# Two graph-attention layers: the logits of a pair side by side, layer 1's edge weights handled per pair and turned through HBM

## The chip, the cores and the metric

The kernel runs on one NeuronCore of one Trainium2 chip. The metric is the device time of one execution in microseconds (us), lower is better. All arithmetic is fp32. Five instruction streams matter: the PE (TensorE: matmuls and transposes into PSUM), DVE (VectorE), ACT (ScalarE), POOL (GpSimd) and SP, the queue that issues nearly all DMAs. Each executes its own list strictly in the order in which it was written.

## The reference, cut to what matters

x is 128 batches of 128 nodes with 512 features, adj 128 batches of a 128 x 128 integer matrix. Layer 0 is masked attention with 8 heads of 64, layer 1 a graph attention with one head:

```python
q, k, v = x @ Wq + bq, x @ Wk + bk, x @ Wv + bv            # 8 heads of 64
attn = softmax(where(adj > 0, q @ k.T / 8, -1e9))          # per batch and head, 128 x 128
x = layernorm(x + relu((attn @ v) @ Wo + bo))
Wh = x @ W
e = leaky_relu((Wh @ a1)[:, None] + (Wh @ a2)[None, :], 0.2)
attention = softmax(where(adj == 0, -1e9, e))              # per batch, 128 x 128
out = layernorm(x + elu(attention @ Wh))
```

The kernel computes `attention @ (x @ W)` as `(attention @ x) @ W`, and gets `Wh @ a1` and `Wh @ a2` from two vectors `W @ a` that it folds once at the start.

## The kernel before

**Tiling.** The 128 batches are worked on as 64 pairs; pair p is batches 2p and 2p+1. The products with Wq, Wk, Wv, Wo and W take the pair's two batches as the two rows of blocks of one 2 x 2 block product, and do it with 7 block products in place of 8 (`PRODUCTS`, L137; the sums of blocks that this needs are `left_sums`, L145, for the left side and `weight_sums`, L129, for the weights). The seven products go to three PSUM banks A, B and C, which accumulate one upon the other: a bank is read by DVE or ACT between two products (`qk_p1`, `qk_p6`, `v_p6`, `w_p6`, `o_c11` and so on), and the PE may only add the next product when that read is done. Here `qk` is the product with Wq and Wk together, `v`, `o` and `w` are those with Wv, Wo and W; `qk3` is the fourth product of `qk`.

**Stages of a pair.** `load_blocks` and `x_transpose` bring x in transposed form. `qk0` to `qk6` and `v0` to `v6` follow. `logits` (L396) writes 128 x 1024 logits of one batch to two PSUM banks, `mask_logits` and `max_logits` (DVE), `exp_logits` and `norm_logits` (ACT) make the softmax. The weights are then transposed: DVE turns 32 x 32 blocks (`weights_t`, L437), a DMA writes the result to HBM (`weights_out`, L443), four DMAs read it back in transposed block order (`weights_in`, L448). `mix_values` (L456) multiplies by v into one PSUM bank, and ACT copies it out. After `o`, `residual0`, `stats0` to `norm0` make the layer norm. The edge stage of layer 1 works batch by batch: `edge_term` (dot products with the folded vectors), `edge_row` (a PE transpose of a broadcast column), `edge_sums`, `edge_leaky`, `edge_mask`, `edge_max`, `edge_exp`, then `edges_t` (L525), a PE transpose of the 128 x 128 weights, and `edges_t_out` (L529), its copy by ACT. `mix_nodes` (L533), `w0` to `w6`, the elu, a residual and the second layer norm finish the pair, and `store` writes it.

**What sets the order.** `PLAN` (L19) gives each step a due time relative to its pair; step k of pair p gets the key `p * PERIOD + PLAN[k]`, all are sorted, and the queues are filled in that order (L574 to L625). The plan's numbers are therefore only an order: the place of a step within a period is its value modulo `PERIOD`, and the number of whole periods in it says how many pairs later than `logits` it comes. Before, `mix_values` to `mix_nodes` of a pair come one period after its logits, and `w` two periods after.

**PSUM.** There are 8 banks: `ps_att` has one buffer of two banks for logits (L80), `ps_acc` the banks A, B, C (L81), `ps` three buffers of one bank (L82) that `mix_values`, `edge_row`, `edges_t`, `mix_nodes` and the folding share.

**Order on the PE before**, within one period in the steady state: `mix_nodes`, `logits0`, both `mix_values`, `logits1`, then `v4` to `v6`, `w` and `o` interleaved, `qk`, with the `edge_row` and `edges_t` transposes among `qk` and the `v0` to `v3` of the next pair.

**Loads of weights.** `load_block_x` (L122) issues two DMAs per 256 x n block, each for 128 partitions, with a source of 4 x 32 rows. Wq and Wv are issued from ACT's queue, all else from SP's (L170 to L184).

Of the kernel before, what the change touches and what calls it, by code (L numbers as in the profile page):

```python
# [17 lines left out]
PERIOD = 80.36  # L18
PLAN = dict(  # L19
    load_blocks=-203.35, load_adj=-141.65, x_transpose0=-108.79, x_transpose1=-80.72, sums_qk=-62.62, mask=-35.32,  # L20
    sums_v=-33.81, x_sums=-30.87, qk0=-30.03, qk_p1=-28.89, qk1=-24.47, qk_p1q=-23.84, qk_p6=-23.67, qk4=-22.15,
    qk3=-21.47, qk2=-20.46, qk_p7=-19.06, qk_c11=-17.42, qk_c22=-16.69, qk5=-15.77, v0=-13.29, sums_fold0=-12.95,
    v_p1=-11.35, fill_logits1=-10.97, qk6=-9.66, qk_c21=-9.52, v1=-8.33, v2=-7.72, v_p6=-6.99, v3=-6.55,
    fill_logits0=-4.19, qk_c12=-2.81, sums_o=-1.37, logits0=0.0, v_p7=1.78, mask_logits0=6.87, logits1=6.98,
    v4=8.58, v_c11=11.52, max_logits0=11.75, mask_logits1=12.17, v_c22=12.53, v5=17.32, max_logits1=17.42,
    v_c21=18.18, v6=18.57, v_c12=18.66, exp_logits0=26.37, sum_logits0=28.64, exp_logits1=31.22, norm_logits0=33.91,
    fill_edges0=36.7, sums_fold1=37.99, sums_fold_t0=42.14, sum_logits1=47.8, load_x0=56.09, norm_logits1=56.91,
    weights_t0=57.44, sums_fold_out0=60.06, weights_out0=61.6, weights_in0=62.47, sums_fold_t1=65.58,
    weights_t1=67.46, sums_fold_out1=74.55, mix_values0=81.46, weights_out1=82.7, weights_in1=84.68,
    mix_values1=87.22, mix_values_out0=94.58, mix_values_out1=96.97, sums_w=98.84, o_sums=103.62, o0=108.53,  # L30
    load_x1=109.41, o_p1=114.18, fill_edges1=114.73, o1=117.76, o_p1l=118.1, o2=120.61, o_p6=122.66, o3=122.75,
    o_p7=123.47, o4=123.68, o_c11=126.83, o_c22=129.32, o5=129.79, o_c21=130.83, residual01=132.36, o6=132.67,
    o_c12=133.46, stats01=133.46, mean01=133.56, residual00=134.07, rstd01=136.55, stats00=137.12, shift01=137.46,
    mean00=137.78, norm01=137.87, rstd00=137.95, edge_term01=138.68, edge_term11=139.19, shift00=140.27,
    norm00=141.75, edge_term10=142.12, edge_term00=142.31, edge_row1=143.18, edge_sums1=143.88, edge_row0=145.26,
    edge_leaky1=147.3, edge_sums0=147.37, edge_mask1=149.05, edge_leaky0=150.02, edge_max1=150.22,
    edge_mask0=151.47, edge_max0=152.05, edge_exp1=152.16, edge_exp0=152.23, edge_norm1=152.34, edges_t1=152.35,
    edges_t0=154.18, edges_t_out1=154.18, edge_norm0=154.29, mix_nodes1=154.39, edges_t_out0=154.42,
    mix_nodes0=154.6, mix_nodes_out1=156.09, mix_nodes_out0=157.89, z_sums=164.73, w0=173.41, w1=179.87,
    w_p1=181.52, w_p6=182.07, w2=182.1, w3=185.01, w_p7=187.54, w4=187.83, w_c11=188.88, w_c22=190.51, w5=195.11,  # L40
    w6=195.64, w_c21=198.1, elu_exp1=198.84, w_c12=200.38, elu_low1=215.59, elu_max1=222.2, elu_exp0=222.5,
    elu_low0=228.48, residual11=235.55, elu_max0=240.61, stats11=243.8, mean11=247.72, rstd11=249.46,
    residual10=251.29, shift11=265.27, stats10=269.96, mean10=297.04, finish1=299.37, rstd10=315.64, store1=320.24,
    shift10=323.36, finish0=332.2, store0=341.53)
# [4 lines left out]
    xb=2, adj=4, xT=3, sx=2, pr=2, e1a512=1, e1b512=1, mask=1, u2512=1, u3512=2, qT=2, kT=2, e1a256=2, cv=2,  # L49
    u2256=1, u3256=1, t=2, scr=2, cw=4, prb=1, prT=2, oT=2, x=2, at=3, so=1, e1b256=2, co=5, e=2, attT=7, zT=2,  # L50
# [4 lines left out]
def tile_two_graph_layers(ctx: ExitStack, tc: tile.TileContext, x, adj, wq, bq, wk, bk, wv, bv, wo, bo, w, a, out,  # L55
# [24 lines left out]
    ps_att = ctx.enter_context(tc.tile_pool(name="ps_att", bufs=1, space=bass.MemoryType.PSUM))  # L80
    ps_acc = ctx.enter_context(tc.tile_pool(name="ps_acc", bufs=1, space=bass.MemoryType.PSUM))  # L81
    ps = ctx.enter_context(tc.tile_pool(name="ps", bufs=3, space=bass.MemoryType.PSUM))  # L82
# [6 lines left out]
    XB, PRB, PRD, NMEAN = {}, {}, {}, {}  # L89
# [32 lines left out]
    def load_block_x(t, k, queue, src, rows, cols):  # L122

        for c in range(2):
            queue.dma_start(t[:, k, c, :], bass.AP(
                tensor=src.tensor, offset=src.offset + 32 * (2 * rows + c) * D + cols.start,
                ap=[[P * D, 4], [D, 32], [1, cols.stop - cols.start]]))
# [48 lines left out]
    load_blocks(1)  # L176
    load_adj(1)
    wv_b, wo_b, w_b = (block_weight(n, HALF) for n in ("wv", "wo", "w"))
    for t, src, queue, load in ((wv_b, wv, nc.scalar, load_block_x), (wo_b, wo, nc.sync, load_block),
                                (w_b, w, nc.sync, load_block)):  # L180
        load(t, 0, queue, src, 0, lo)
        load(t, 5, queue, src, 0, hi)
        load(t, 1, queue, src, 1, lo)
        load(t, 2, queue, src, 1, hi)  # L184
# [211 lines left out]
    def logits(p, i):  # L396
        b = 2 * p + i
        q, k = (QK[m, b].rearrange("r (h n) -> r h n", n=P) for m in "qk")
        ST["s", b] = ps_att.tile([P, 2, H // 2, P], F32, tag="att", name=f"s_{b}")
        for hp in range(H // 2):  # L400
            for j in range(2):
                r = slice(j * DH, (j + 1) * DH)
                nc.tensor.matmul(ST["s", b][:, j, hp, :], q[r, hp, :], k[r, hp, :], start=True, stop=True)  # L403
# [33 lines left out]
    def weights_t(b):  # L437

        PRB[b] = buf([P, 4, H, 32], F32, "prb", f"prb_{b}")
        nc.vector.transpose(PRB[b].rearrange("p k h s -> p h k s"),  # L440
                            PR.pop(b).rearrange("p h (k r) -> p h k r", r=32))

    def weights_out(b):  # L443

        PRD[b] = hbm.tile([P, 4, H * 32], F32, tag="prd", name=f"prd_{b}")
        nc.sync.dma_start(PRD[b], PRB.pop(b).rearrange("p k h s -> p k (h s)"))

    def weights_in(b):  # L448

        PRT[b] = buf([P, 4, H, 32], F32, "prT", f"prT_{b}")  # L450
        prd = PRD.pop(b)
        for k in range(4):
            nc.sync.dma_start(PRT[b][32 * k:32 * k + 32].rearrange("r v h s -> r v (h s)"),
                              prd[:, k, :].rearrange("(v r) e -> r v e", v=4))
# [31 lines left out]
    def edge_term(b, s):  # L486
        store = (EI, EJ)[s]
        store[b] = small.tile([P, 1], F32, tag=f"e{s}", name=f"e{s}_{b}")
        scr = buf([P, D], F32, "scr", f"scr{s}_{b}")
        nc.vector.scalar_tensor_tensor(scr, X1[b], 1.0, wa_bc[s], op0=ALU.mult, op1=ALU.mult, accum_out=store[b])  # L490


    def edge_row(b):
        ST["j", b] = ps.tile([P, P], F32, tag="ps", name=f"pj_{b}")
        nc.tensor.transpose(ST["j", b], EJ.pop(b).to_broadcast([P, P]), ident)

    def fill_edges(b):
        AT[b] = buf([P, P], F32, "at", f"at_{b}")
        nc.gpsimd.memset(AT[b], NEG)

    def edge_sums(b):
        ST["e", b] = buf([P, P], F32, "e", f"e_{b}")
        nc.scalar.activation(ST["e", b], ST.pop(("j", b)), AF.Identity, bias=EI.pop(b), scale=1.0)

    def edge_leaky(b):
        e = ST["e", b]
        nc.vector.scalar_tensor_tensor(e, e, ALPHA, e, op0=ALU.mult, op1=ALU.max)

    def edge_mask(p, i):
        b = 2 * p + i  # L510
        nc.vector.copy_predicated(AT[b], ADJ[p][:, i, :], ST.pop(("e", b)))

    def edge_max(b):
        NMAX["e", b] = small.tile([P, 1], F32, tag="nmax1", name=f"nmax1_{b}")
        nc.vector.tensor_reduce(NMAX["e", b], AT[b], AX.X, ALU.max, negate=True)

    def edge_exp(b):
        TOT["e", b] = small.tile([P, 1], F32, tag="tot1", name=f"tot1_{b}")
        nc.scalar.activation(AT[b], AT[b], AF.Exp, bias=NMAX.pop(("e", b)), scale=1.0, accum_out=TOT["e", b])

    def edge_norm(b):
        RI[b] = small.tile([P, 1], F32, tag="ri", name=f"ri_{b}")
        nc.vector.reciprocal(RI[b], TOT.pop(("e", b)))

    def edges_t(b):  # L525
        ST["at", b] = ps.tile([P, P], F32, tag="ps", name=f"pat_{b}")
        nc.tensor.transpose(ST["at", b], AT.pop(b), ident)

    def edges_t_out(b):  # L529
        ATT[b] = buf([P, P], F32, "attT", f"attT_{b}")  # L530
        nc.scalar.copy(ATT[b], ST.pop(("at", b)))

    def mix_nodes(b):  # L533

        attT = ATT.pop(b)
# [13 lines left out]
    def elu_exp(b):  # L549
        t = buf([P, D], F32, "t", f"t_{b}")  # L550
        ST["t", b] = t
        nc.scalar.activation(t, Y[b], AF.Exp, scale=RI[b])  # L552
# [5 lines left out]
    def elu_max(b):  # L558
        nc.vector.scalar_tensor_tensor(Y[b], Y[b], RI.pop(b), ST.pop(("t", b)), op0=ALU.mult, op1=ALU.max)
# [21 lines left out]
    for p in range(n_pair):  # L581
        if p > 1:
            at("load_adj", p, load_adj, p)
            at("load_blocks", p, load_blocks, p)
        at("x_sums", p, x_sums, p)
# [64 lines left out]
```

## Time and profile before

| | |
|---|---|
| time, median of 3 runs | 2511.69 us (2510.5 to 2513.35) |
| span of the profiled execution | 2509.6 us, mean granted PE clock 0.989 |
| busy: PE | 2413.6 us, 96% |
| busy: DVE, ACT, POOL | 1912.0, 1607.5, 1459.9 us |
| share of 16 DMA engines used by SP's queue | 32.3% |
| first `logits` matmul | 60.1 us after the start |
| last pair's first `logits` matmul | 2425.2 us |

The page divides the span into 40 slices and gives each engine's busy share per slice in tenths. A row of the timeline gives the start, the length, the engine, the line, the operation with output and inputs, the shape and how many instructions were merged; in brackets stands how long the engine was idle before and what released it. A row of the waits gives the waiting group, what it waited for, the total in us, how often, and the longest. fp32 matmuls appear as two records each. The end of a PE record is modelled, so the distance from one start to the next is the better measure.

### The profile page before, as it was taken

To read this page: it belongs to the slowest core of one execution; us is meant where nothing else is said; L and a number is where in the kernel's file an instruction comes from. 1 tells how busy PE (TensorE), PEld (TensorE's weight loads), DVE (VectorE), ACT (ScalarE), POOL (GpSimd) and SP (SyncE) were. 2 spreads that over 40 slices of the span, in tenths; PEclk is the share of its full clock that TensorE was granted. 3 is DMA by queue.
4 is the path that set the end of the run, shared out by engine and by line. 5 is a ranking of instruction groups with operands and counts; after the bars stand their busy time and mean duration, and the time that the engine had idled before them with its cause. 6 is when DMAs were issued, how large, how long until landed. Compare 5 with 4: busy or idle time off the path is not lost.

```text
span 2509.6 us, 51523 instructions
## 1 busy us (share of the span) xinstructions
PE 2413.6 (96%) x17928; PEld 2190.1 (87%) x17928; DVE 1912.0 (76%) x4031; ACT 1607.5 (64%) x5635; POOL 1459.9 (58%) x2053
## 2 busy tenths in 40 slices
PE   3999999999999999999999999999999999999995
PEld 3898998998998998998998898998988988989984
DVE  3777877877877877877877877877777877878775
ACT  0666666666666666676666666666666666666663
POOL 2356656656656656656656656556556556556554
PEclk8999999999999999999999999999999999999997
DMA  4323323423323323323423423323323323333222
GB/s 133 110 78 98 122 84 102 121 78 108 121 83 104 114 89 104 120 86 101 122 79 106 121 78 108 115 82 110 106 88 113 106 83 118 96 93 119 86 73 72
DMA packets 221076, 252.69 MB, mean 101 GB/s; under 512 B 19920, under 2 KB 170448, under 8 KB 220816
## 3 DMA queue, kind: packets, MB, share of 16 engines
q1 hardware_dynamic: 218896, 246.49, 32.3%
q8 instruction: 144, 2.36, 0.4%
q10 hardware_dynamic: 1584, 2.10, 0.2%
q14 instruction: 116, 0.95, 0.1%
q0 software_dynamic: 336, 0.79, 0.1%
HBM read 148.64 MB, written 100.66 MB: 99 GB/s over the span
## 4 chain that ended last, share of the span: by engine, by line
PE 83%; DMA 7%; DVE 6%; SPq 1%; ACT 1%; issue 1%; POOL 0%; ACTq 0%; POOLq 0%; DVEq 0%
PE pBqk L257 10%; PE pAqk L257 8%; PE pCqk L257 7%; PE pBw L246 7%; PE pBo L246 7%; PE pBv L246 6%; PE pCv L246 5%; PE s L403 5%; PE pAw L246 4%; PE pCw L246 4%; PE pAo L246 4%; PE pCo L246 4%; PE po L462 4%; PE pAv L246 3%; PE pz L538 3%; DMA prT<-prd 3%
## 5 line engine op out<-in xcount | busy, mean ns | idle before, releaser
L556 POOL TENSOR_SCALAR t<-t 128x512 f32<-128x512 f32 x126 | 255.0, 2024 | 414.7 <-ACT t L552 414.7
L426 ACT ACTIVATE pr<-pr,nmax 128x128 f32<-128x128 f32 x1024 | 396.0, 391 | 4.3 <-DVE nmax L420 4.3
L435 ACT ACTIVATE pr<-pr,tot 128x128 f32<-128x128 f32 x1024 | 313.8, 412 | 1.4 <-DVE tot L430 1.4
L257 PE MATMUL pBqk<-sx,wqk 128*128 128x128 f32 x2048 | 251.4, 276 | 22.3 <-DVE wqk L132 19.2
L257 PE MATMUL pAqk<-xT,wqk 128*128 128x128 f32 x2048 | 251.3, 276 | 19.1 <-DVE xT L288 19.1
L257 PEld LDWEIGHTS pBqk<-sx,wqk 128*128 128x128 f32 x2048 | 245.3, 193 | 26.1 <-issue 21.6
L273 POOL TENSOR_SCALAR rstd<-mv 128x1 f32<-128x1 f32 x256 | 81.3, 318 | 318.9 <-DVE mv L270 309.5
L257 PEld LDWEIGHTS pAqk<-xT,wqk 128*128 128x128 f32 x2048 | 245.4, 193 | 22.3 <-DVE xT L288 19.1
L415 DVE COPY_PREDICATED pr<-mask,s 128x1024 f32<-128x1024 int32 x128 | 173.5, 1355 | 112.0 <-PE s L403 112.0
L257 PE MATMUL pCqk<-sx,wqk 128*128 128x128 f32 x2048 | 250.0, 275 | 0.0
L257 PEld LDWEIGHTS pCqk<-sx,wqk 128*128 128x128 f32 x2048 | 244.6, 192 | 3.3
L301 ACT ACTIVATE e1aqk<-pAqk,bk 128x128 f32<-128x128 f32 x256 | 73.1, 368 | 246.1 <-PE pAqk L257 246.1
L426 ACT ACTIVATION_READ_ACCUMULATOR pr<-pr,nmax 128x1 f32 x1024 | 194.6, 190 | 0.0
L490 DVE SCALAR_TENSOR_TENSOR scr<-co,wa_bc 128x512 f32<-128x512 f32 x256 | 188.6, 773 | 1.9 <-ACT co L281 1.9
L274 POOL TENSOR_TENSOR rstd<-rstd,half 128x1 f32<-128x1 f32 x256 | 153.0, 597 | 21.3
L562 POOL TENSOR_TENSOR cw<-cw,co 128x512 f32<-128x512 f32 x126 | 160.0, 1270 | 0.0
L420 DVE TENSOR_REDUCE nmax<-pr 128x8 f32<-128x1024 f32 x128 | 155.7, 1216 | 2.2
L440 DVE STREAM_TRANSPOSE prb<-pr 128x1024 f32<-128x1024 f32 x128 | 156.4, 1222 | 0.6 <-DMA prd<-prb 0.6
L462 PE MATMUL po<-prT,cv 128*64 128x128 f32 x2048 | 134.4, 278 | 22.0 <-DMA prT<-prd 16.4
L278 POOL TENSOR_SCALAR nmean<-mv,rstd 128x1 f32<-128x1 f32 x256 | 135.4, 529 | 26.2
L471 ACT ACTIVATE oT<-po,bv 128x128 f32<-128x128 f32 x512 | 142.7, 383 | 12.1 <-PE po L462 11.5
L403 PE MATMUL s<-kT,qT 64*128 64x128 f32 x2048 | 148.7, 285 | 1.5 <-DVE pr L415 1.5
(150 smaller groups left out, 6155.3 us busy)
## 6 DMA issues: line engine op xcount, KB each, us to landing
prd<-prb SPq DMA_DIRECT2D x128, 512.0 KB
prT<-prd SPq DMA_DIRECT2D x512, 128.0 KB
xb<-in_x_dram SPq DMA_DIRECT2D x256, 128.0 KB
x<-in_x_dram SPq DMA_DIRECT2D x128, 256.0 KB
out_dram<-cw SPq DMA_DIRECT2D x128, 256.0 KB
adj<-in_adj_dram SPq DMA_DIRECT2D x64, 128.0 KB
wqk<-in_L_gnn_Wq_dram ACTq DMA_DIRECT2D x4, 256.0 KB
wv<-in_L_gnn_Wv_dram ACTq DMA_DIRECT2D x8, 128.0 KB
```

The costliest lines, as they stand in the source:

```text
L246: nc.tensor.matmul(out, left_block(left, blk.pair, a_i, c), weight[:, b_i, c, :], start=first and c == 0, stop=j in LAST and c == 1, skip_ ...
L257: nc.tensor.matmul(out[:, f * P:(f + 1) * P], weight[:, b_i, c, f * P:(f + 1) * P], left_block(left, blk.pair, a_i, c), start=first and f ...
L403: nc.tensor.matmul(ST["s", b][:, j, hp, :], q[r, hp, :], k[r, hp, :], start=True, stop=True)
L415: nc.vector.copy_predicated(PR[b], MASK[p][:, i, :].unsqueeze(1).to_broadcast([P, H, P]), ST.pop(("s", b)).rearrange("p j h k -> p (j h) k"))
L420: nc.vector.tensor_reduce(NMAX[b], PR[b], AX.X, ALU.max, negate=True)
L426: nc.scalar.activation(PR[b][:, h, :], PR[b][:, h, :], AF.Exp, bias=nmax[:, h:h + 1], scale=1.0, accum_out=TOT[b][:, h:h + 1])
L435: nc.scalar.activation(PR[b][:, h, :], PR[b][:, h, :], AF.Copy, scale=tot[:, h:h + 1])
L440: nc.vector.transpose(PRB[b].rearrange("p k h s -> p h k s"), PR.pop(b).rearrange("p h (k r) -> p h k r", r=32))
L462: nc.tensor.matmul(ST["o", b][j * DH:(j + 1) * DH, hp, :], v[:, h * DH:(h + 1) * DH], prT[:, :, j * (H // 2) + hp, :], start=True, stop=True)
L490: nc.vector.scalar_tensor_tensor(scr, X1[b], 1.0, wa_bc[s], op0=ALU.mult, op1=ALU.mult, accum_out=store[b])
L556: side_engine(b // 2).tensor_scalar(t, t, 1.0, -1.0, op0=ALU.min, op1=ALU.add)
L562: side_engine(b // 2).tensor_tensor(Y[b], Y[b], X1.pop(b), op=ALU.add)
```

## The change

It does five things.

1. **Logits of a pair adjacent.** `logits` now does both batches in one step, and `ps_att` gets two buffers (four banks), so that the second batch's logits need not wait until the first's were read. `ps` is cut to one buffer for this.
2. **Layer 1's edges per pair.** `edge_row` to `edge_norm` handle both batches in one step. The masking, leaky relu, maximum, fill and reciprocal are one instruction of 256 columns in place of two of 128; the ACT steps and the `edge_row` transposes stay two.
3. **Edge weights turned through HBM.** For all pairs but the last, `edges_t` is one DVE 32 x 32 block transpose of 128 x 256 in place of two PE transposes, `edges_t_out` is a DMA to HBM, and a new `edges_t_in` reads back with four DMAs in runs of 128 bytes. ACT's copies fall away. The last pair keeps the PE. In turn the last pair's attention weights of layer 0 (`weights_t`, `weights_out`) now use PE transposes and copies by DVE and ACT in place of HBM.
4. **Loads of layer 0's weights.** `load_block_x` issues four DMAs of 32 partitions each; the loads of Wv move from ACT's queue to SP's, ahead of pair 1's x.
5. **A new plan** with more distance between a DMA and its reader: the edge stage and `mix_nodes` come two periods after a pair's logits, `w` three. Some buffer counts change.

Order on the PE after, from the new plan modulo its period (number of periods after the pair's logits in brackets): `logits` [0], `mix_values1` [1], `v1`, `v2` [0], `edge_row` [2], `v3`, `v4`, `w0`, `v5`, `v6`, `w1`, `w2`, `w3`, `w4`, `o0`, `w5`, `w6`, `o1`, `o4`, `o3`, `o2`, `o5`, `qk0`, `o6`, `qk1`, `qk2`, `mix_nodes1` [2], `qk3`, `qk4`, `qk5`, `mix_nodes0` [2], `qk6`, `v0`, `mix_values0` [0].

The diff, cut to its core:

```diff
-PERIOD = 80.36
+PERIOD = 75.72
...
-    xb=2, adj=4, xT=3, sx=2, pr=2, e1a512=1, e1b512=1, mask=1, u2512=1, u3512=2, qT=2, kT=2, e1a256=2, cv=2,
-    u2256=1, u3256=1, t=2, scr=2, cw=4, prb=1, prT=2, oT=2, x=2, at=3, so=1, e1b256=2, co=5, e=2, attT=7, zT=2,
+    xb=2, adj=4, xT=2, sx=1, e1a512=1, e1b512=1, u2512=1, pr=2, mask=1, u3512=1, qT=2, kT=2, e1a256=2, t=2, scr=1,
+    cw=6, u2256=1, u3256=2, cv=2, prb=2, x=2, prT=2, oT=2, so=1, e1b256=1, co=6, at=2, e=1, atb=1, attT=1, zT=2,
...
-    ps_att = ctx.enter_context(tc.tile_pool(name="ps_att", bufs=1, space=bass.MemoryType.PSUM))
+    ps_att = ctx.enter_context(tc.tile_pool(name="ps_att", bufs=2, space=bass.MemoryType.PSUM))
...
-    ps = ctx.enter_context(tc.tile_pool(name="ps", bufs=3, space=bass.MemoryType.PSUM))
+    ps = ctx.enter_context(tc.tile_pool(name="ps", bufs=1, space=bass.MemoryType.PSUM))
...
-        for c in range(2):
-            queue.dma_start(t[:, k, c, :], bass.AP(
-                tensor=src.tensor, offset=src.offset + 32 * (2 * rows + c) * D + cols.start,
-                ap=[[P * D, 4], [D, 32], [1, cols.stop - cols.start]]))
+        for q in range(4):
+            queue.dma_start(t[32 * q:32 * q + 32, k, :, :], bass.AP(
+                tensor=src.tensor, offset=src.offset + (q * P + 64 * rows) * D + cols.start,
+                ap=[[D, 32], [32 * D, 2], [1, cols.stop - cols.start]]))
...
-    load_blocks(1)
-    load_adj(1)
...
-    for t, src, queue, load in ((wv_b, wv, nc.scalar, load_block_x), (wo_b, wo, nc.sync, load_block),
-                                (w_b, w, nc.sync, load_block)):
+    for t, src, load in ((wv_b, wv, load_block_x), (wo_b, wo, load_block), (w_b, w, load_block)):
+        load(t, 0, nc.sync, src, 0, lo)
...
+        if t is wv_b:
+            load_blocks(1)
+            load_adj(1)
...
-    def logits(p, i):
-        b = 2 * p + i
+    def logits(p):
+        for b in (2 * p, 2 * p + 1):
...
     def weights_t(b):
+        if b // 2 == n_pair - 1:
+            ST["w", b] = ps_att.tile([P, H, P], F32, tag="att", name=f"ppT_{b}")
+            for h in range(H):
+                nc.tensor.transpose(ST["w", b][:, h, :], PR[b][:, h, :], ident)
+            return
...
-    def edges_t(b):
-        ST["at", b] = ps.tile([P, P], F32, tag="ps", name=f"pat_{b}")
-        nc.tensor.transpose(ST["at", b], AT.pop(b), ident)
-
-    def edges_t_out(b):
-        ATT[b] = buf([P, P], F32, "attT", f"attT_{b}")
-        nc.scalar.copy(ATT[b], ST.pop(("at", b)))
+    def edges_t(p):
+        if p < n_pair - 1:
+            ATB[p] = buf([P, 2, P], F32, "atb", f"atb_{p}")
+            nc.vector.transpose(ATB[p].rearrange("p i n -> p (i n)"), AT.pop(p).rearrange("p i n -> p (i n)"))
+        else:
...
+    def edges_t_out(p):
+        if p < n_pair - 1:
+            ATD[p] = hbm.tile([2, P, P], F32, tag="atd", name=f"atd_{p}")
+            nc.sync.dma_start(ATD[p].rearrange("i n m -> n i m"), ATB.pop(p))
+
+    def edges_t_in(p):
+        ATT[p] = buf([P, 2, P], F32, "attT", f"attT_{p}")
+        if p < n_pair - 1:
+            atd = ATD.pop(p)
+            for k in range(4):
+                nc.sync.dma_start(ATT[p][32 * k:32 * k + 32].rearrange("r i (v s) -> r (i v) s", s=32),
+                                  atd[:, :, 32 * k:32 * k + 32].rearrange("i (v r) s -> r (i v) s", r=32))
```

On DVE the new plan puts the folding of the second vector, `sums_fold1`, which reads W, ahead of `qk_p6` of the first pair; before, `sums_fold0` came after that pair's `qk` reads and `sums_fold1` a period later.

## The prediction

> **What bounds the kernel now.** First the page. The PE is 96% busy and its row is full from the second slice to the last but one, so it bounds all but the ends. What it costs per pair is read from one period of its timeline, from one `edge_row` transpose (`pj`) to the next.
>
> ```profile
> PE 2413.6 (96%) x17928; PEld 2190.1 (87%) x17928; DVE 1912.0 (76%) x4031; ACT 1607.5 (64%) x5635; POOL 1459.9 (58%) x2053
> PE   3999999999999999999999999999999999999995
> ```
>
> ```profile
> 1807.64 0.27 PE L495 MATMUL pj<-ident,e 128*128 128x128 f32 x1
> ...
> 1810.51 1.95 PE L257 MATMUL pCqk<-sx,wqk 128*128 128x128 f32 x16
> 1812.38 0.33 PE L527 MATMUL pat<-ident,at 128*128 128x128 f32 x1
> 1812.55 1.03 PE L246 MATMUL pBv<-wv,sx 128*128 128x256 f32 x4
> ...
> 1815.17 0.27 PE L527 MATMUL pat<-ident,at 128*128 128x128 f32 x1
> 1815.28 1.95 PE L538 MATMUL pz<-attT,co 128*128 128x128 f32 x16
> 1817.15 1.16 PE L403 MATMUL s<-kT,qT 64*128 64x128 f32 x16
> 1818.25 1.97 PE L462 MATMUL po<-prT,cv 128*64 128x128 f32 x32
> 1820.14 1.16 PE L403 MATMUL s<-kT,qT 64*128 64x128 f32 x16
> 1821.24 1.13 PE L246 MATMUL pCv<-wv,sx 128*128 128x256 f32 x4
> ...
> 1844.99 0.27 PE L495 MATMUL pj<-ident,e 128*128 128x128 f32 x1
> ```
>
> Nothing waits here: 1844.99 - 1807.64 = 37.35 us is the PE's own work on a pair. The first `pj` of pair 6 starts at 334.78 and that of pair 60 at 2378.09, so the mean period is 2043.3 / 54 = 37.84: 0.49 us per pair is lost. The waits name the place, `po` (`mix_values`), for weights from HBM and for v:
>
> ```profile
> PEld po L462 <- ACT cv L377: 18.8, 18, 1.6
> PE po L462 <- DMA prT<-prd: 16.4, 22, 1.5
> ```
>
> The start: the first logits begin at 60.1. The timeline shows loads that come late, and a PE waiting for Wk's sums until 42.08.
>
> ```profile
> 4.49 18.06 ACTq L125 DMA_DIRECT2D wv<-in_L_gnn_Wv_dram  x8
> 18.94 5.28 SPq L125 DMA_DIRECT2D wqk<-in_L_gnn_Wk_dram  x4
> 40.71 1.23 DVE L132 TENSOR_TENSOR wqk<-wqk 128x1024 f32<-128x1024 f32 x1 [6.66 <-DMA wqk<-in_L_gnn_Wk_dram]
> 42.08 3.75 PE L257 MATMUL pBqk<-sx,wqk 128*128 128x128 f32 x16 [19.24 <-DVE wqk L132]
> ```
>
> From the last pair's first logits (2425.2) to the end is 84.4 us. So 2509.6 = 60.1 + 57.8 (two filling periods, to the third pair's logits at 117.8) + 61 x 37.8 + 84.4.
>
> **What the Trainium skill says.** "DMA: Bandwidth & Descriptors", "Why a DMA increments its semaphore by 16 and not by 1": a DMA uses the largest number of engines up to 16 that divides the slowest dimension of both its sides. The old weight load has 128 and 4, so 4 engines; the trace agrees (DMA share 0.26 and 0.27, 99 and 97 GB/s, from 10 to 20 us; 0.84 and 262 GB/s from 45 to 50, when Wo and W come). "TensorEngine Tiling (Array Packing)", "Key Properties": a change of tiling mode drains the PE. The trace agrees: 16 `qk` passes take 1.79, so 16 of `s`, two row tiles side by side, should take 0.89, and take 1.09. "DMA: Bandwidth & Descriptors", "Specifications": runs under 512 bytes are read, modified and written; no run here shows what that costs. "SBUF — State Buffer", "Who interferes with whom": a DVE instruction with two SBUF inputs and a POOL instruction that reads SBUF block each other. `edge_mask` agrees: 254 ns at least, 292 median, 1189 at most.
>
> **The change part by part.**
>
> *PE work.* Without the two `pat`: 0.17 and 0.11 us to the next start, and the product ahead of the first takes 1.87 in place of 1.79: 0.33 us a pair gone. The order of modes was full, `s`, `po`, `s`, full; it becomes full, `po`, `s s`, `po`, full: as many switches. Two `s` with one overhead save 0.2, the split `po` (1.89 for 32 passes against 32 x 0.056 = 1.79) adds 0.1. So 37.35 - 0.33 - 0.1 = 36.9, say 36.95; the bounds are 36.8 and 37.15, if the switches cost what they save.
>
> *Waits in the period.* I walk the new order with the PE never idle, 0 at `logits`, 0.2 us from a PE end to a reader and 0.1 back. From the timeline, a DVE instruction costs its duration less 0.08 when another follows.
> - One `ps` buffer. `mix_values0` ends as `logits` begins; ACT's four copies take about 1.2, the pair's logits 2.0: 0.6 to spare. `mix_values1` ends at 2.95, `v1` and `v2` give 1.8, and ACT (`elu_exp0`, then 1.2 of copies) is done at 4.4; `edge_row` is due at 4.8. The two `mix_nodes` have 5.4 between them for a 0.59 copy.
> - DVE from `qk6` to `w_p6`, which `w3` waits for: `qk_c12`, stats, two `edge_term`, a mean, two masks and maxima of 1.28 + 1.14, `edge_leaky`, `edge_mask`, `edge_max`, `x_transpose1` and seven reads of 0.34 to 0.42 make 12.1 to 12.9 with both latencies, the upper end with a blocked `edge_mask`. The PE has `v0`, `mix_values0`, the logits, `mix_values1`, `v1`, `v2`, `edge_row` and seven products of 0.86, 12.9. Slack 0 to 0.8.
> - Bank A: `o_c11` has 0.15 to spare ahead of `qk0`, ACT's eight `qk` copies (2.2) 0.1 to 0.2 ahead of `qk2`.
> None loses by itself, all are tight: 0.2 us a pair, from 0 to 0.8 if three slip.
>
> *Edges through HBM.* `edges_t` on DVE ends near 13, the DMA out (2.7 to 3.7 us for 512 KB before) near 16, SP issues four reads at 0.43, landing 3.3 later: 21. `mix_nodes1` is due at 26. The added 256 + 1024 packets at the page's mean (32.3% of 16 x 2509.6 us / 218896 packets = 59 ns) are 4.7 us of 16 engines a pair; twice that, for the short runs, still lands near 24. Nothing is lost, at worst 1 to 2 us. What stands behind the reads on SP, `load_adj` and `weights_out0`, is not needed until after 21.
>
> *Softmax weights.* `weights_t0` ends on DVE near 21.5, `weights_t1` near 27.7, the reads of the first land near 33.3, `mix_values0` is due at 35.9: 2.6 of slack. The 0.49 lost today goes.
>
> *DVE and ACT* lose some 0.4 and 0.5 us a pair; neither sets the period: no gain. So a period is 36.95 + 0.2 = 37.15.
>
> *Start.* 16 engines: x 0.5, Wq, Wk, Wv 1 MB each, x of pair 1, Wo, W make 6.3 MB; at 218 to 262 GB/s (40 to 50 us today) that is 24 to 29, about 30 with the 50 issues of 0.45 on SP in front. Wk is in near 13. But DVE's `sums_fold1` needs W, the last load, and stands before `qk_p6`, which holds `qk3`. It took 3.5 us for one vector today. So 34 for that, then `qk_p6` 0.7, four products 7.2, `v0` 0.9, `qk_c12` 0.7, some 2 of half clock: first logits at 45 (40 to 55), from 60.1.
>
> *Filling.* Three periods now. Period 0 is bound by softmax and DMA, 25.6 today, say 27; period 1 has 28.6 of PE work, say 30; period 2 has 30.7, say 32. Fourth pair's logits at 45 + 89 = 134.
>
> *End.* From 84.4, the last pair's HBM round (second `prb` at 2452.4 to its `po` at 2462.2, 9.8) shrinks to some 2, a fourth stage's emptying adds about 2: 78 (72 to 86).
>
> Sum: 134 + 60 x 37.15 + 78 = 2441; with the 2 us between span and time, 2444 us.
>
> **The rivals.**
> - *The queues give it back.* Three tight places slip, on average 0.3 each: 37.05 + 0.9 = 37.95 a pair, 2491. For it: slack of 0.1 to 0.4 everywhere, one `ps` buffer for five users, POOL blocking DVE. Against it: today's order also has `v` waiting on DVE 0.2 us at a time, and loses nothing more by that.
> - *Only the ends gain.* The PE work stays at 37.35 as the switches eat the transposes, with 0.25 of waits: 37.6, 2470. For it: no row shows `s` after `po` after a full product. Against: fewer records.
> - *Slower.* The 128-byte reads land 2 to 3 us later than reckoned, `mix_nodes1` waits in every period, SP's queue hands the delay to `weights_out0`: 37.15 + 1.6 = 38.75, with a start at 55: 2549. For it: the unknown price of short runs, and SP's strict order. Against it: SP's DMAs use only a third of the engines, and the plan leaves 3 to 5 us.
>
> **How the numbers follow.** Forecast 0.60, only the ends 0.13, queues 0.14, slower 0.13. The predicted time is the forecast's 2444. The low end takes the floor at 36.9 and the end at 72, with a start at 41: about 2418. The high end reaches over both middle rivals to 2502. Faster by over 0.2% (under 2506.7) comes from the first three, less a little: 0.84; same 0.03; slower 0.13.
>
> **What would show it.** No `pat` but the last pair's; `pj` to `pj` at 37.0 to 37.3; no wait of `po` for `prT`; first logits at 45, DVE waiting for W before it; the last stretch near 78. Wrong would be: a PE wait for `attT`'s DMA, for `w_p6`, `o_c11` or ACT's copies out of `ps` at each pair, or first logits after 55.

## The result, and the profile after

The changed kernel takes 2441.19 us (median of 4 runs, 2439.77 to 2441.88) against 2511.1 us before (4 runs beside it, 2507.96 to 2513.35): a ratio of 0.9722, 95% interval 0.9705 to 0.9739. The profiled execution has a span of 2440.1 us, 69.5 less than before.

First the page of the changed kernel: busy times, and the slices.

```profile
PE 2383.7 (98%) x17818; PEld 2156.8 (88%) x17818; DVE 1881.5 (77%) x3838; ACT 1570.9 (64%) x5510; POOL 1497.0 (61%) x1989
...
PE   4999999999999999999999999999999999999996
```

The PE still bounds all but the ends, with 110 records and 29.9 us of busy time less. DVE and ACT lost some 31 and 37 us of work; neither is the bound, and the run with DVE's merged steps undone shows below what that work is worth. One period of the PE's timeline in the changed kernel, from one `edge_row` to the next:

```profile
1209.07 2.06 PE L402 MATMUL s<-kT,qT 64*128 64x128 f32 x32
1211.06 1.09 PE L475 MATMUL po<-prT,cv 128*64 128x128 f32 x16
...
1213.91 0.38 PE L515 MATMUL pj<-ident,e 128*128 128x128 f32 x2
...
1219.31 1.03 PE L244 MATMUL pAw<-w,zT 128*128 128x256 f32 x4
1220.17 1.09 PE L244 MATMUL pBw<-w,sz 128*128 128x256 f32 x4
1221.11 1.03 PE L244 MATMUL pCw<-w,sz 128*128 128x256 f32 x4
...
1235.10 1.06 PE L580 MATMUL pz<-attT,co 128*128 128x128 f32 x8
...
1244.99 1.09 PE L475 MATMUL po<-prT,cv 128*64 128x128 f32 x16
1246.01 2.06 PE L402 MATMUL s<-kT,qT 64*128 64x128 f32 x32
...
1250.85 0.38 PE L515 MATMUL pj<-ident,e 128*128 128x128 f32 x2
```

No row carries a bracket, so no wait is long enough to be listed, and 1250.85 - 1213.91 = 36.94 us is a period: 0.41 below the 37.35 of before. The mean is read from the fourth pair's first logits to the last pair's, in the changed kernel and then in the kernel before:

```profile
49.64 2.06 PE L402 MATMUL s<-kT,qT 64*128 64x128 f32 x32
...
137.56 2.06 PE L402 MATMUL s<-kT,qT 64*128 64x128 f32 x32
...
2354.64 2.06 PE L402 MATMUL s<-kT,qT 64*128 64x128 f32 x32
```

```profile
60.08 1.16 PE L403 MATMUL s<-kT,qT 64*128 64x128 f32 x16
...
156.14 1.16 PE L403 MATMUL s<-kT,qT 64*128 64x128 f32 x16
...
2425.17 1.16 PE L403 MATMUL s<-kT,qT 64*128 64x128 f32 x16
```

It is 2217.08 / 60 = 36.95, against (2425.17 - 156.14) / 60 = 37.82. So the loss between floor and mean, 0.47 a pair before, is gone. The edge weights' way through HBM is seen on SP's queue:

```profile
1221.73 0.38 SPq L562 DMA_DIRECT2D atd<-atb  x1
1222.16 0.46 SPq L103 DMA_DIRECT2D x<-in_x_dram  x1
1223.60 1.80 SPq L570 DMA_DIRECT2D attT<-atd  x4
1225.45 0.45 SPq L99 DMA_DIRECT2D adj<-in_adj_dram  x1
```

The page's list of DMA issues gives 1.8 and 1.9 us from issue to landing for them (last column), so the last read, issued at about 1225, is in near 1227. `mix_nodes1`, which reads it, starts at 1235.10: some 8 us to spare.

```profile
prd<-prb SPq DMA_DIRECT2D x126, 512.0 KB, 2.9
prT<-prd SPq DMA_DIRECT2D x504, 128.0 KB, 3.6
...
atd<-atb SPq DMA_DIRECT2D x63, 128.0 KB, 1.8
attT<-atd SPq DMA_DIRECT2D x252, 32.0 KB, 1.9
```

At the start, Wk's sums now begin at 15.25 and 17.49 instead of 32.82 and 40.71. The first logits start at 49.64 in place of 60.08. What holds them is that DVE waits for W, and the PE for DVE. The list of waits shows the first; the PE's 13.7 us it puts down to no releaser ("issue"):

```profile
PE pBqk L255 <- issue: 13.7, 1, 13.7
DVE wa_scr L207 <- DMA w<-in_L_gnn_W_dram: 12.8, 3, 10.9
```

The timeline shows the second: the last pieces of the fold (`wa_scr`) start when W has come, the read `qk_p6` (`u2qk`) follows the fold, and the PE's next product follows that read.

```profile
36.09 0.43 DVE L207 SCALAR_TENSOR_TENSOR wa_scr<-w,a_bc 128x256 f32<-128x256 f32 x1 [1.36 <-DMA w<-in_L_gnn_W_dram]
...
38.03 0.68 DVE L314 TENSOR_TENSOR u2qk<-pBqk,e1aqk 128x512 f32<-128x512 f32 x1
38.82 3.75 PE L255 MATMUL pBqk<-sx,wqk 128*128 128x128 f32 x16 [13.75 <-issue]
```

**Where the 69.5 us went.** First logits 10.4 earlier. From there to the fourth pair's logits 87.9 us against 96.1 before (156.14 - 60.08), 8.1 less. Sixty periods of 36.95 in place of 37.82: 52.0 less, 24.6 of it floor and 27.4 waits. The last stretch is 85.5 against 84.4: 1.1 more.

### The profile page after: what moved, and what is told of

The parts are those of the page before. It is cut to its first block, busy times and chain, and to the rows that moved or that the text cites. A ratio compares the mean times of both kernels' runs of the same rounds, so it can differ in the third digit from the quotient of the medians.

```text
span 2440.1 us, 51873 instructions
## 1 busy us (share of the span) xinstructions
PE 2383.7 (98%) x17818; PEld 2156.8 (88%) x17818; DVE 1881.5 (77%) x3838; ACT 1570.9 (64%) x5510; POOL 1497.0 (61%) x1989
## 3 DMA queue, kind: packets, MB, share of 16 engines
q1 hardware_dynamic: 304528, 261.98, 40.4%
## 5 line engine op out<-in xcount | busy, mean ns | idle before, releaser
L271 POOL TENSOR_SCALAR rstd<-mv 128x1 f32<-128x1 f32 x256 | 112.0, 437 | 319.7 <-DVE mv L268 310.2
L604 POOL TENSOR_TENSOR cw<-cw,co 128x512 f32<-128x512 f32 x126 | 184.3, 1482 | 163.2 <-DVE cw L601 163.2
L255 PE MATMUL pBqk<-sx,wqk 128*128 128x128 f32 x2048 | 253.1, 277 | 18.6 <-issue 13.7
L255 PE MATMUL pAqk<-xT,wqk 128*128 128x128 f32 x2048 | 251.9, 277 | 13.2 <-DVE xT L286 10.5
L598 POOL TENSOR_SCALAR t<-t 128x512 f32<-128x512 f32 x126 | 245.4, 1948 | 31.5 <-ACT t L594 31.5
L279 ACT ACTIVATE co<-co,nmean,rstd 128x512 f32<-128x512 f32 x128 | 104.2, 814 | 246.8 <-DVE kT L330 216.8
L506 DVE SCALAR_TENSOR_TENSOR scr<-co,wa_bc 128x512 f32<-128x512 f32 x256 | 201.8, 788 | 8.4 <-ACT co L279 3.2
L410 POOL MEMSET pr<- 128x1024 f32 x128 | 121.6, 951 | 99.8 <-DVE prb L444 99.8
L272 POOL TENSOR_TENSOR rstd<-rstd,half 128x1 f32<-128x1 f32 x256 | 159.5, 623 | 21.3
L314 DVE TENSOR_TENSOR u2qk<-pBqk,e1aqk 128x512 f32<-128x512 f32 x64 | 44.2, 690 | 144.3 <-PE pBqk L255 141.6
L150 POOL TENSOR_TENSOR sx<-sx,xT 128x256 f32<-128x256 f32 x63 | 46.1, 732 | 175.6 <-DVE xT L286 175.5
```

The costliest lines, as they stand in the source:

```text
L255: nc.tensor.matmul(out[:, f * P:(f + 1) * P], weight[:, b_i, c, f * P:(f + 1) * P], left_block(left, blk.pair, a_i, c), start=first and f ...
L272: nc.gpsimd.tensor_tensor(RSTD[key], RSTD[key], half, op=ALU.pow)
L410: nc.gpsimd.memset(PR[b], NEG)
L598: side_engine(b // 2).tensor_scalar(t, t, 1.0, -1.0, op0=ALU.min, op1=ALU.add)
L604: side_engine(b // 2).tensor_tensor(Y[b], Y[b], X1.pop(b), op=ALU.add)
```

## The experiments

Each kernel is the changed kernel with one edit, or the kernel before with one edit where that is said. Ratios are against the kernel before, run beside it.

### The weights' loads as before

```diff
-        for q in range(4):
-            queue.dma_start(t[32 * q:32 * q + 32, k, :, :], bass.AP(
...
+        for c in range(2):
+            queue.dma_start(t[:, k, c, :], bass.AP(
...
+                ap=[[P * D, 4], [D, 32], [1, cols.stop - cols.start]]))
...
+    load_blocks(1)
+    load_adj(1)
...
+    for t, src, queue, load in ((wv_b, wv, nc.scalar, load_block_x), (wo_b, wo, nc.sync, load_block),
```

> The changed kernel with the loads of Wq, Wk, Wv as before: two DMAs of 4 x 32 source rows per block, Wv on ACT's queue, pair 1's x and adj ahead of it; all else as changed. Theory (the loads matter, and W, last in SP's queue, holds DVE's folding and so the first pair's fourth qk product): W comes at 52 to 53 as in the kernel before, the folding ends near 56, first logits near 68 in place of 49.6, time 2441 + 18 = 2459. Rival 1 (only Wk's arrival matters, which was 32.8 and 40.7 in the kernel before and 15 to 17.5 now): first logits near 60, time 2451. Rival 2 (a late start is made up in the filling periods): under 2445. The steady period stays 36.95 in all.

Measured: 2458.86 us, ratio 0.979 (0.9775 to 0.9805). The first logits are at 67.21; the period stays 36.94.

```profile
PE pAqk L255 <- DVE xT L286: 21.6, 1, 21.6
PE pBqk L255 <- DVE wqk L130: 19.3, 1, 19.3
PE pBqk L255 <- issue: 6.3, 1, 6.3
```

The loads are worth 17.7 us of the total. That is more than the 10.4 by which the start is shorter: with the old loads the new order's fold still waits for W, and the first logits are 7.1 later than before's (Wk's sums themselves are 2.2 later, at 35.06 and 42.90). The plan gave part of the loads' gain back.

### Layer 1's vectors folded after the first logits

```diff
-    ... sums_fold1=-29.39 ...
+    ... sums_fold1=25.0 ...
```

> The changed kernel with one number of the plan changed: sums_fold1 from -29.39 to 25.0, so that DVE no longer waits for W ahead of qk_p6 of the first pair but folds in period 0. Theory: the PE's wait of 13.7 us ahead of pair 0's fourth qk product goes, first logits at 36 to 38 in place of 49.6, of which period 0 gives back 0 to 3: time 2429 to 2432, faster than both kernels. Rival (the x of pair 1, Wv or the softmax chain of pair 0 hold the start anyway): first logits at 45 or later, or period 0 longer by as much; time 2437 to 2441.

Measured: 2428.67 us (2428.47 to 2430.54), ratio 0.9671 (0.9657 to 0.9686), faster than both kernels, 12.5 us under the changed one. First logits at 31.58: 18 us earlier, better than expected, and the wait of DVE for W before `qk_p6` is gone. The wait was only 13.7; most of the rest is that the PE also runs faster. Without the idle time every 16 passes of `qk` from 21.68 on take 1.79, where the two groups after the wait take 3.54 and 2.74 in the changed kernel. But the first period takes 32.5 us in place of 26.9 (logits at 31.58 and 64.08), with a new wait:

```profile
PE pAqk L255 <- ACT pr L434: 5.9, 1, 5.9
```

The list names ACT, but the last thing to end before the PE starts at 45.98 is the second half of the second pair's `x_transpose` on DVE, at 45.84: the fold, which runs from 40.45 to 45.06, stood ahead of it.

```profile
45.18 0.66 DVE L286 STREAM_TRANSPOSE xT<-xb 128x512 f32<-128x512 f32 x1
45.98 3.45 PE L255 MATMUL pAqk<-xT,wqk 128*128 128x128 f32 x16 [5.91 <-ACT pr L434]
```

So 18.1 were won and 5.6 given back.

### The fold behind the second pair's transpose

```diff
-    ... sums_fold1=-29.39 ...
+    ... sums_fold1=40.3 ...
```

> The changed kernel with sums_fold1 on DVE after x_transpose0 and sum_logits0 of the first pair (due 40.3 in place of -29.39). With the fold at 25.0 the first logits came at 31.58, but the first period took 32.5 us in place of 26.9, since the fold stood ahead of the sums of the first softmax and of the next x_transpose. Theory: behind those it no longer holds them, first logits at 31.6, first period 28 to 30, time 2424 to 2427. Rival: the first period is held by the softmax weights' round, or the fold delays the second batch's half of it, so the period stays near 32 and the time near 2428.7.

Measured: 2427.84 us (2426.84 to 2428.98), ratio 0.969 (0.9672 to 0.9708): not to be told from the one before. First logits at 32.95, first period 30.49, just outside what was expected; the time is what the rival said. The wait has only moved:

```profile
PE pwa L217 <- DVE wa_rep L211: 3.3, 1, 3.3
```

DVE now does both folds in one go, from 42.50 to 52.2, and the second pair's `qk_p6` waits behind them until 53.43. The first period is 3.6 longer than the changed kernel's, a little less than one fold takes on DVE (4.3 us alone, 5.4 where others slow it). What the later fold saves is thus the waiting for W; most of its own work stays on the path while the pipeline fills.

### Both folds in period 1

```diff
-    ... sums_fold1=-29.39 ... sums_fold0=44.28 ... sums_fold_t1=51.88, sums_fold_out1=51.93 ...
+    ... sums_fold1=100.7 ... sums_fold0=100.0 ... sums_fold_t1=110.0, sums_fold_out1=110.1 ...
```

> The changed kernel with both folds of W a moved to period 1 (sums_fold1 100.7, sums_fold0 100.0, their transposes and copies at 110 to 112). Theory: as with the one fold moved, first logits at 31.6; and period 0, which took 32.5 there and 26.9 as changed because both folds (9 us of DVE) stood between the softmax's steps, takes 25 to 27: time 2428.7 less 5 to 8 = 2421 to 2424. Rival (period 0 is held by the softmax and its HBM round alone, or period 1 takes up the folds' time): within 2 us of 2428.7.

In this kernel the folds read W after `sums_w` has overwritten one of its blocks with a sum, so the two folded vectors are of other numbers; the amount of work is the same. Measured: 2436.84 us, ratio 0.9709 (0.9693 to 0.9725). First logits at 31.37, first period 26.0, but the second takes 43.7 in place of 29.3:

```profile
PE pwa L217 <- DVE wa_rep L211: 10.5, 1, 10.5
```

The fold's transpose stood in the PE's queue while DVE was still folding; all behind it waited. Worse than the two above, and outside both theory and rival: the time only moved to another period, since the transpose's place in the PE's order was not given time for the fold.

### The edges turned by the PE again

```diff
-        if p < n_pair - 1:
+        if p < 0:
```

(in `edges_t`, `edges_t_out` and `edges_t_in`, so that all pairs go the last pair's way)

> The changed kernel with the edge weights of every pair turned by two PE transposes and one ACT copy, as the last pair's are, in place of DVE, HBM and back. Theory (the PE's own work is the period, so its instructions are paid for in full): steady period 36.95 + 0.33 = 37.28, up to 37.35 (the measured difference of the two clean periods is 0.41), time 2441 + 21 to 26 = 2462 to 2467. Rival 1 (the gain came from the waits for DMA alone): within 5 us of 2441. Rival 2 (the single PSUM buffer, now with one more user, makes the PE wait): period over 37.6, time over 2480.

Measured: 2455.08 us, ratio 0.9778 (0.9762 to 0.9795): 13.9 us more than the changed kernel. The period is 37.16, and the two transposes cost 1042.26 - 1042.04 = 0.22 us:

```profile
1042.04 0.38 PE L557 MATMUL pat<-ident,at 128*128 128x128 f32 x2
1042.26 1.03 PE L244 MATMUL pCw<-w,sz 128*128 128x256 f32 x4
```

Less than expected. Before, the two stood apart: 0.17 and 0.11 to their next starts, and the product ahead of the first stretched by 0.09, 0.37 in all. Adjacent they cost 0.11 each, 0.22 of the 0.37. The other 0.15 is a wait in the kernel before that is too short for a bracket. There the PE's weight load for the first transpose starts with its matmul and not ahead of it, 0.05 after ACT has ended `edge_exp` on the weights that it turns:

```profile
1812.14 0.19 ACT L519 ACTIVATION_READ_ACCUMULATOR at<-at,nmax 128x1 f32 x1
1812.38 0.14 PEld L527 LDWEIGHTS pat<-ident,at 128*128 128x128 f32 x1
```

These 0.05 us return in 63 of that trace's 64 pairs. So the clean period of before holds a wait for ACT that the new order no longer has.

### Edge steps of DVE per batch again

```diff
-        nc.vector.copy_predicated(AT[p], ADJ[p], ST.pop(("e", p)))
+        e = ST.pop(("e", p))
+        for i in range(2):
+            nc.vector.copy_predicated(AT[p][:, i, :], ADJ[p][:, i, :], e[:, i, :])
```

(`edge_leaky` and `edge_max` likewise)

> The changed kernel with edge_leaky, edge_mask and edge_max as two DVE instructions of 128 columns each in place of one of 256; all else as changed. Theory 1 (DVE does not set the period, so merging gained nothing, as predicted): period 36.95, time within 3 us of 2441. Theory 2 (in the walk the reads on DVE up to w_p6 have no slack left: w_p6's read ends at 1220.02 and w3 starts at 1220.17, 0.07 us late): every tenth of a us more on DVE there is paid for by the PE; the three pairs cost some 0.2 us more (0.39 for 0.34, 0.5 for 0.44, 0.4 for 0.33), period 37.1 to 37.2, time 2450 to 2456.

Measured: 2444.14 us (2442.62 to 2444.67), ratio 0.9735 (0.972 to 0.9749), 3 us more, between the theories and nearer to the first. The period is 1245.80 - 1208.79 = 37.01, 0.07 more, and no wait is listed in the steady state. The loss shows only as a longer distance between rows:

```profile
1217.30 1.08 PE L244 MATMUL pCv<-wv,sx 128*128 128x256 f32 x4
1218.22 1.03 PE L244 MATMUL pBw<-w,sz 128*128 128x256 f32 x4
```

0.92 to the next start where the changed kernel has 0.86; and `pBw` before `pCw` takes 0.94 in both (1219.95 to 1220.89 here, 1220.17 to 1221.11 there). DVE is thus a few hundredths late already in the changed kernel. The merging is not free of effect, because the slack is nearly nil.

### One buffer for the logits, the new order

```diff
-    ps_att = ctx.enter_context(tc.tile_pool(name="ps_att", bufs=2, space=bass.MemoryType.PSUM))
+    ps_att = ctx.enter_context(tc.tile_pool(name="ps_att", bufs=1, space=bass.MemoryType.PSUM))
...
-    ps = ctx.enter_context(tc.tile_pool(name="ps", bufs=1, space=bass.MemoryType.PSUM))
+    ps = ctx.enter_context(tc.tile_pool(name="ps", bufs=3, space=bass.MemoryType.PSUM))
```

(the last pair's softmax weights go through HBM, for want of banks)

> The changed kernel with one buffer for logits and three for ps, as before, and the last pair's softmax weights through HBM (with one buffer that pair's transposes can't be placed); the order stays as changed. Theory: the second batch's logits wait until DVE has masked the first's (the mask ends 1.65 us after the first's logits end), which stands on the PE's path in every pair: period 36.95 + 1.6 to 1.8 = 38.5 to 38.8, time 2535 to 2555, slower than before. So the pair's logits can only be adjacent with two buffers, and the fewer ps buffers are their price. Rival (the three ps buffers save waits that make up for part of it): period under 38.2, time under 2520.

Measured: 2555.2 us, ratio 1.0177 (1.0162 to 1.0192), slower than before. The period is 1071.24 - 1032.54 = 38.70.

```profile
PE s L402 <- DVE pr L414: 95.8, 64, 1.5
```

Every pair waits 1.5 us until DVE has masked the first batch's logits. The second buffer is what makes the adjacent order pay: without it, that order takes 112 us more than with it (2555.2 - 2442.7, the time of the last kernel below, which treats the last pair alike), though it has three `ps` buffers again.

### Before, with `v4` between the logits and the weights' product

The kernel before, with the first product after the logits moved ahead of `mix_values`:

```diff
-    v4=8.58, v_c11=11.52, ...
+    v4=4.0, v_c11=11.52, ...
```

> The kernel before with one number of the plan changed: v4 from 8.58 to 4.0, so that the fifth v product stands between the two mix_values and the second has 0.86 us more for its weights to come from HBM. Theory (the 0.49 us a pair that the kernel before lost over its clean period of 37.35 are mix_values waiting for the weights' DMA): most of the waits, 0.3 to 1.5 us each, go; period 37.4 to 37.6, time 2511 less 15 to 28 = 2483 to 2496. Rival 1 (the loss has another cause, so it stays): 2508 to 2512. Rival 2 (the order of bank C's reads now makes v4 or DVE wait): slower than 2511.

Measured: 2553.99 us, ratio 1.0171 (1.0156 to 1.0186), slower. The wait for `prT` fell from 16.4 us (22 times) to 2.3 (3), but the move made another, larger one:

```profile
PE pBw L246 <- DVE cv L390: 25.5, 61, 0.4
```

Also the PE's order then changes tile shape more often, and the period is 38.45. This run doesn't settle what the wait for the weights was worth; the next one was made for that.

### Before, without the round through HBM

The kernel before, from the second pair on without the DMAs of the softmax weights; their product reads the first pair's weights instead, so all later pairs' attention is that of the first.

```diff
+        if b >= 2:
+            PRB.pop(b)
+            return
         PRD[b] = hbm.tile([P, 4, H * 32], F32, tag="prd", name=f"prd_{b}")
...
+        if b >= 2:
+            PRT[b] = PRT0[b % 2]
+            return
```

> The kernel before without the HBM round of the softmax weights: from pair 1 on weights_out and weights_in are left out, and mix_values multiplies by pair 0's weights; DVE's transposes stay. It leaves out that part of the computation, for the time alone. Theory (the 0.49 us a pair lost over the clean period are waits for this DMA): the period falls to 37.35 to 37.45, the filling and the end shorten by the rounds in them (2 to 10 us): time 2511 - 28 - 2 to 10 = 2470 to 2483. Rival 1 (other waits take their place): period 37.7 or more, 2495 to 2508.

Measured: 2480.92 us (2480.23 to 2481.68), ratio 0.9882 (0.9867 to 0.9897), 32 us less than before beside it (2512.69).

```profile
1016.44 1.16 PE L403 MATMUL s<-kT,qT 64*128 64x128 f32 x16
...
1053.79 1.16 PE L403 MATMUL s<-kT,qT 64*128 64x128 f32 x16
```

Every period is the floor, 37.35; the mean from the fourth pair's logits (157.07) to the last pair's (2398.32) is 37.35 too. So the loss of before, 0.47 a pair, was the softmax weights' round. (The edit removes the transfers as well as the wait, so it doesn't tell lateness of this round from its load on the engines.) The last stretch is 2479.9 - 2398.32 = 81.6, only 2.8 less than before's 84.4, although the last pair has no round either.

### The last pair's softmax weights through HBM

```diff
-        if b // 2 == n_pair - 1:
+        if b // 2 == n_pair:
```

(in `weights_t`, `weights_out` and `weights_in`)

> The changed kernel with the last pair's softmax weights turned through HBM like all others, in place of PE transposes and copies by DVE and ACT. The prediction said that the HBM round of 9.8 us shrinks to some 2, so the end is 8 us shorter by this edit. If so: last pair's first logits to the end 85.5 + 8 = 93 us, time near 2449. Rival: the last mix_values waits for the emptying stages anyway (one ps bank, the mix_nodes of pair 61 ahead of it), so that most of the round lies beside other work: 86 to 90 us, time 2441 to 2446. All else as in the changed kernel.

Measured: 2442.74 us, ratio 0.9751 (0.9736 to 0.9766); by the medians 1.6 us more than the changed kernel. The last pair's first logits start at 2352.62 of a span of 2440.4: a last stretch of 87.8 against 85.5, so the PE's transposes there bring 2.3 and not 8. (The six other runs of the changed kernel that keep them and the two logits buffers have last stretches of 84.8 to 85.5.) The timeline of this kernel around the last pair's `mix_values`:

```profile
2375.69 1.16 PE L580 MATMUL pz<-attT,co 128*128 128x128 f32 x8 [1.12 <-ACT zT L585]
2382.17 1.97 PE L475 MATMUL po<-prT,cv 128*64 128x128 f32 x16 [5.32 <-DMA prT<-prd]
2385.37 1.97 PE L475 MATMUL po<-prT,cv 128*64 128x128 f32 x16 [1.23 <-ACT oT L484]
```

And the changed kernel's own:

```profile
2375.53 2.05 PE L441 MATMUL ppT<-ident,pr 128*128 128x128 f32 x16
2377.46 1.13 PE L580 MATMUL pz<-attT,co 128*128 128x128 f32 x8
2379.26 1.16 PE L580 MATMUL pz<-attT,co 128*128 128x128 f32 x8 [0.68 <-ACT zT L585]
2381.81 1.09 PE L475 MATMUL po<-prT,cv 128*64 128x128 f32 x16 [1.38 <-ACT zT L585]
2384.58 1.09 PE L475 MATMUL po<-prT,cv 128*64 128x128 f32 x16 [1.68 <-ACT oT L484]
```

The round through HBM costs a wait of 5.32, but it replaces 1.93 of PE transposes (2375.53 to 2377.46) and a wait of 1.38 on the single `ps` bank, which is emptied by ACT between each two products. Most of the round lay beside work that must be done anyway. The times alone leave the size open: the medians are 1.6 us apart, but the kernel before took 2506.03 beside this run, 5 less than beside the changed kernel, so by the ratios it would be 7. The last stretches, read in the traces, don't depend on that.

## Why the prediction was right, and where it was not

The forecast case held: 2441.19 against 2444, and its mechanism with it; that the number came so close was luck, as its terms show one by one:

- **PE work, 36.95: right, with other shares.** The floor is 36.94, 0.41 below. The prediction took 0.33 for the transposes (its own three figures add up to 0.36) and 0.1 for the changes of mode. The trace of before gives 0.37 for the transposes with the products about them; the run with the PE's transposes back shows that 0.22 of it is theirs, and 0.15 was a short wait for ACT in a period of which the prediction said "Nothing waits here". That leaves 0.04 for the modes. What the modes cost can be read from the rows' starts: `v0`, 16 passes of `po`, 32 of `s`, 16 of `po` and `v1` take 0.96 + 1.02 + 1.99 + 1.02 + 0.97 = 5.96, and 5.30 at the rate of products among their like (0.86 for a `v`, 1.79 for 32 passes): 0.66 in excess (the traces show the excess, not a drain as such). The same sum for the order of before gives 0.69. So the direction was right, and the shares of the transposes and of the modes were smaller than reckoned.
- **Stalls, 0.2 a pair: none beyond the floor.** The mean is 36.951 and the floor 36.94, so 60 periods were 12 us shorter than forecast. The mechanism, all places tight, holds (`u2w`, the read `w_p6`, ends at 1220.02 and the product behind it starts at 1220.17, some hundredths late, which the floor holds; the run with unmerged edge steps loses 0.07). But tight on every pair is not late, and places with positive slack do not add up to a loss. The 0.2 was a middle of a range without a mechanism behind it.
- **Softmax weights: right.** No wait for `prT` is left in the steady state, and the run without the round shows that this round was the whole loss of before.
- **Edges through HBM: right, with more room than reckoned.** Reads land 1.9 us after their issue, not 3.3 or more; slack 8 us, not 5. "DMA: Bandwidth & Descriptors", "Specifications", of the Trainium skill speaks of reading, modifying and writing for runs under 512 bytes. No delay from it shows here: 252 reads in runs of 128 bytes land faster than those of `prT`, which move four times as much each (longer runs of the same size were not tried). The whole round takes 1.3 us of the 16 engines a pair, not the 4.7 reckoned from the mean packet: SP's queue has 40.4% of 2440.1 us, and 36.8% of 2453.3 with the PE's transposes back. The rival that was slower than before rested on this and falls.
- **DVE and ACT, no gain: nearly right.** 3 us of 70 is DVE's merged edge steps. `edge_mask` of 256 columns takes 444 ns in the mean, where half of it took 663 before. The place did that and not the merging: with the steps per batch again, but in the new order, the half takes 298. That the rest of the 663 was POOL's blocking, as the prediction has it, fits; no run took POOL's work away.
- **Start, 45: 4.6 too short in this trace.** The mis-sized term is "So 34 for that": the fold was to end at 34 us and ended at 38.0 (`u2qk`, the read behind it, starts at 38.03). Two things went otherwise than reckoned, and neither was tried alone. The bytes moved at 201 to 217 GB/s from 20 us on, a little under the 218 to 262 assumed; and Wk's eight issues took 8.9 us on SP's queue, 1.11 each and not 0.45, at a time when the engines were full (DMA share 0.89 from 0 to 10 us and 1.08 from 10 to 20), so that W's issues ended only at 32.2. From the fold's end to the logits it took 11.6, against 11.5 added up. (The fold's pieces also start 0.47 apart where they started 0.35 apart before; `scr`, which they write, has one buffer in place of two. No run gave it the second again.) Some 2 us of the 4.6 belong to this execution: four other traces with the same loads and the same place of the fold have `u2qk` at 36.8 to 37.2 and the first logits at 47.4 to 48.7. That 16 engines work and not 4 is borne out: from 10 to 20 us the share was 0.26 before and is 1.08 now.
- **Filling, 89: right** (87.9, as 26.9, 29.3 and 31.7 against 27, 30 and 32). Most of the 8.1 us gained there needs the second logits buffer: with one, in the new order, the filling takes 142.14 - 47.40 = 94.7.
- **End, 78: 7.5 too short.** The step that failed is "shrinks to some 2". The HBM round of 9.8 lay for the most part beside the emptying of the earlier pairs, and its removal brought 2.3 (and at most 2.8 in the kernel before, in the run without any round). The four-stage emptying costs, from 84.4 to 87.8 without that edit, 3.4 and not 2; the one `ps` bank, with ACT's copies between its users, is seen in its waits.

So +4.6, -1.1, -12 and +7.5 nearly cancel. The total was better than its parts, by luck: each end was read too favourably and the steady state too badly.

**The rivals.** That the queues give it back falls with a steady state free of waits; that only the ends gain falls with the floor of 36.94, and the ends gained less than the middle (10.4 + 8.1 - 1.1 = 17.4 against 52.0).

What stays open: which part of the new plan, the order or the longer distances, took away the 27.4 us of waits, since no run has one without the other; and whether a fold split into shorter pieces between the second pair's reads could save part of the 3.6 us that the later fold adds to the first period. Neither was tried.

## What to carry to other kernels

An order with the PE never idle can be worth as much as the operations taken away from it: here 27 of 70 us were losses of half a microsecond per pair to a DMA round, 14 the PE's transposes, and one extra PSUM buffer was the condition for the better order. A period without listed waits can still hold some: 0.15 us a pair were found only by the start of a weight load. For ends, count only what is last there: a removed round of 10 us brought 2, because most of it lay beside other work, and an early piece of work that needs the last load (the fold, which needs W) held the first logits back by 18 us, some 13 of them in the total. Before adding a small loss for each tight place, walk the places; here each had slack or was some hundredths late, and the sum was nearly zero.

## What the runs showed of the hardware

- Reads in runs of 128 bytes: four DMAs of 32 KB land 1.9 us after issue; with 512 KB written and read per batch beside them, SP's queue has 40.4% of the engines' time, against 36.8% without this round, and no wait for it is listed.
- PE transposes of fp32, 128 x 128, cost 0.11 us each in the stream, adjacent or alone between products (`pj` and the second `pat` of before). The first `pat` of before took 0.17, behind the wait for ACT.
- The PE ran slowly after a long idle time: 16 passes of `qk` that take 1.79 us in the steady state took 3.54 after the 13.75 us gap at 38.82, the next 16 took 2.74, at a granted clock of 0.50 from 30 to 38 us and 0.73 from 38 to 50. In the four other traces with this gap (12.5 to 13.2 us) the two groups took 3.24 to 3.55 and 1.78 to 2.75. So the wait cost 1.4 to 2.7 us more than its length; where the fold came later and the PE did not idle there, these passes took 1.79.
- A DMA's issue can take more than twice as long: 1.11 us each on SP's queue for Wk's eight (DMA share 0.89 from 0 to 10 us, 1.08 from 10 to 20), against 0.47 for W's eight (0.78 from 20 to 30, 0.86 from 30 to 38). That the full engines are the cause is not shown.
